# New orders in the scan, the projections and between the batches of a four-layer kernel

## The chip, the cores and the metric

The kernel runs on 1 core of one Trainium2 chip. The metric is the device time of one execution in microseconds (us), and three runs of the kernel before gave 5660.36, 5663.77 and 5664.23 us. One further execution was taken by the hardware profiler; its times are used for the working. The engines are called as in the profile: PE is TensorE's matmul, PEld its weight load, DVE is VectorE, ACT is ScalarE, POOL is GpSimd, SP is SyncE, whose queue issues most DMAs here. A "q" behind an engine (SPq) is that engine's sequencer, issuing a DMA or waiting.

## The reference

All arrays are float32; the activation x has the shape [4, 128, 128, 128] (batch, rows, columns, channels). Four layers follow each other, each with a residual and a group norm over four channels in front:

```python
x = x + _L0_conv_ref(_gn(x), w_off, b_off, w_def)   # deformable 3x3 convolution, relu
x = x + _L1_conv_ref(_gn(x), W)                     # a scan over the rows
x = x + _L2_conv_ref(_gn(x), Wself, Wm, Wk)         # three products that use sums over rows, columns
x = x + _L3_conv_ref(_gn(x), ...)                   # gated triangle product
```

Layers 1 to 3, cut to what the change touches:

```python
def step(carry, row):                               # layer 1: row after row
    new = row + relu(conv1d_same(carry, W))         # 9 taps, 128 to 128 channels
    return (new, new)

z = einsum('bmkd,hd->bmkh', x, Wself) \
    + einsum('bmd,hd->bmh', x.sum(2), Wm)[:, :, None] \
    + einsum('bkd,hd->bkh', x.sum(1), Wk)[:, None]  # layer 2

xn = layer_norm(x)                                  # layer 3
left = (xn @ left_w + left_b) * sigmoid(xn @ lgate_w + lgate_b)
right = (xn @ right_w + right_b) * sigmoid(xn @ rgate_w + rgate_b)
out_gate = sigmoid(xn @ ogate_w + ogate_b)
out = einsum('bkjd,bkid->bijd', left, right)
out = (layer_norm(out) * out_gate) @ to_out_w + to_out_b
```

## The kernel before

The program has three stages that hardly overlap. `deform_layer` computes layer 0. It ends with a test whether some offset was larger than one (`far`, L757 to L769); a branch on it, `tc.If`, would run a general version instead. `scan_layer` computes layer 1. `message_and_triangle` computes layers 2 and 3, batch after batch. In all three the order on every engine is the order in which the program writes the instructions down (`manual_schedule`), so an instruction that waits holds whatever stands behind it on its engine.

The scan works on one row of all 4 batches at a time, 128 rows in all; a carry tile holds the row split into three column phases and the three sums of phases (L1141 to L1143, `kept` 3 to 5). Per row PE does 18 convolution products into `edge_ps` and `m_ps` (L1081) and four transposes of the next row (L1061); ACT copies one product (L1111) and scales the next row (L1068); DVE combines the products (L1117 to L1134: e, y0, the new phase 0, f, y2, phase 2, e+f, y1, phase 1), makes the three sums, adds the residual into `x2c` (L1145) and takes statistics of it (`stats`, L1150); POOL adds the row to `sum_h` (L1148). Every fourth row SP stores four batches to `x2T`. After the last row DVE sums all statistics (L1154 to L1157).

Then the weights of the last layers are loaded by ACT's and SP's queues, folded and multiplied into `wcat` (L1196 to L1251), and `prelude(0)` makes the factors of layer 2's norm (mean, variance, `ws`, messages `z`). `sums_of(b)` computes layer 2 into the tile X, four rows of x2 in one step: one product of 512 columns on PE (L1359), four additions on DVE into X (L1370), one squaring on ACT (L1377). x2 comes in pieces of 32 rows, 2 MB, into two buffers R (`fetch`, L1347); a piece is fetched into a buffer after the last product that read it. `turned(b, g)` scales and transposes 32 columns of X and counts them; ahead of it `kept_columns` stores the raw columns to `x3d` (L1431; group 0 in `means`, group g+1 in the third block of group g). `spread(b, g)` norms them and makes the gate, stored to `gates`.

`projected(b, q, ...)` makes a quarter q of left and right: 8 columns in one block, 8 products (L1539), a sigmoid on ACT (L1543), two multiplications on DVE (L1545) into L and R[q % 2], written with channel steps of 128 elements. `triangle(b, q)` multiplies R and L per channel (L1557, ACT copies the result into L as L4, L1561). The R buffers thus serve the projections and x2 in turn.

At the turn from a batch to the next the order is: quarter 3 of the projections woven with triangle 2 and `prelude(b + 1)`; `fetch`; triangle 3 by itself; `counted_out(b, 0)` (statistics of the output, L1572, then the factors) woven with the first 6 steps of the next batch's `sums_of` and `turned` (the list `ahead`, 47 steps); `given(b)` woven with the rest. `given` gives the output: its step k stores the result of k-3, loads the gate of k+1 and the x3 columns of k (SP, L1638, L1586, L1591; three buffers each), norms four columns (DVE, ACT), transposes and scales (L1615, L1617), multiplies by the gate on POOL (L1618), and multiplies by `outw` on PE (L1629). `weave` interleaves lists in proportion to their lengths.

Of the kernel before, what the change touches and what calls it, by code (L numbers as in the profile page):

```python
# [19 lines left out]
B = 4  # L20
# [12 lines left out]
DQ = P // NQ  # L33

# [145 lines left out]
def deform_layer(tc, c, small, x, w_off, b_off, w_def, x1, tabs, offs):  # L180
# [14 lines left out]
    with ExitStack() as ctx:  # L195
# [552 lines left out]
        for _ in convs:  # L748
            pass
        count(len(to_count))  # L750
        beside["norms"].append(x1_norm(B - 1, stats))
        while step(B, S):
            pass


# [4 lines left out]
        nc.vector.scalar_tensor_tensor(most, ends[:, 1:2], -1.0, ends[:, 0:1], ALU.mult, ALU.max)  # L760
        most_ps = ps_g.tile([1, 2 * NL], F32, name="most_ps", tag="gn_ps")
# [7 lines left out]
        nc.vector.tensor_copy(far, row)  # L769
        return norms, far  # L770
# [240 lines left out]
def scan_layer(tc, c, small, x1, w, norms, x2T):  # L1011
# [4 lines left out]
    WP = N + 5  # L1016
    counted = small.tile([P, B, 2], F32, name="counted2")
    sum_w = small.tile([P, B, S], F32, name="sum_w")
    sum_h = small.tile([P, B, S], F32, name="sum_h")
    with ExitStack() as ctx:  # L1020
# [5 lines left out]
        ps_m = ctx.enter_context(tc.tile_pool(name="l1ps_m", bufs=1, space=PSUM))  # L1026

        stats = wp.tile([P, B, S, 6], F32, name="stats2")
# [14 lines left out]

        carry = [wp.tile([P, 2 * PHASES, B, WP], F32, name=f"carry_{i}") for i in range(2)]
# [40 lines left out]

        order = {getattr(mybir.EngineType, e) for e in ("PE", "Activation", "DVE", "Pool", "SP")}
        ctx.enter_context(tc.manual_schedule(engines=order))
        chunks = {0: rows(0), RB: rows(RB)}
        px = turned(0)
        ready = {0: (px, scaled(px))}  # L1090
        add, less = ALU.add, ALU.subtract
        for y in range(S):
# [7 lines left out]
            if y:  # L1100
                pa = ps_a.tile([P, B, N + 1], F32, name="edge_ps")
                product(pa, [(less2, old[:, 0], 1), (taps[:, 0], old[:, 2], 0)])
                ps = {}
                for name, wgt, at in (
                    ("m1", taps[:, 1], 1), ("m01", both["w12"], 3), ("m12", both["w01"], 4),
                    ("m012", both["w012"], 5),
                ):
                    ps[name] = ps_m.tile([P, B, N], F32, name=f"{name}_ps")
                    product(ps[name], [(wgt, old[:, at], 1)])
                m1 = two.tile([P, B, N], F32, name="m1")  # L1110
                nc.scalar.copy(m1, ps["m1"])  # L1111
            if y + 1 < S:
                pn = turned(y + 1)
                ready[y + 1] = (pn, scaled(pn))
            if y:
                e = two.tile([P, B, N], F32, name="e")
                nc.vector.tensor_tensor(e, ps["m01"], m1, less)  # L1117
                y0 = two.tile([P, B, N], F32, name="y0")
                nc.vector.tensor_tensor(y0, pa[:, :, 0:N], e, add)  # L1119
                nc.vector.scalar_tensor_tensor(  # L1120
# [3 lines left out]
                nc.vector.tensor_tensor(f, ps["m12"], m1, less)  # L1124
                y2 = two.tile([P, B, N], F32, name="y2")
                n2 = COUNT[2]
                nc.vector.tensor_tensor(y2[:, :, 0:n2], f[:, :, 0:n2], pa[:, :, 1 : 1 + n2], less)
                nc.vector.scalar_tensor_tensor(  # L1128
                    kept(new, 2), y2[:, :, 0:n2], 0.0, part(rt, 2), ALU.max, add
                )  # L1130
                nc.vector.tensor_tensor(e, e, f, add)
                y1 = two.tile([P, B, N], F32, name="y1")
                nc.vector.tensor_tensor(y1, ps["m012"], e, less)  # L1133
                nc.vector.scalar_tensor_tensor(  # L1134
# [5 lines left out]
            if y + 1 < S:  # L1140
                nc.vector.tensor_tensor(kept(new, 3, N), kept(new, 0, N), kept(new, 1, N), add)  # L1141
                nc.vector.tensor_tensor(kept(new, 4, N), kept(new, 1, N), kept(new, 2, N), add)
                nc.vector.tensor_tensor(kept(new, 5, N), kept(new, 3, N), kept(new, 2, N), add)  # L1143
            for p in range(PHASES):
                nc.vector.tensor_tensor(  # L1145
                    x2c[:, :, i, p:S:PHASES], part(px, p), kept(new, p), add
                )
            nc.gpsimd.tensor_tensor(sum_h, sum_h, x2c[:, :, i], add)  # L1148
            for b in range(B):
                nc.vector.bn_stats(stats[:, b, y, :], x2c[:, b, i])  # L1150
# [3 lines left out]
        nc.vector.tensor_tensor(sum_w, stats[:, :, :, 1], stats[:, :, :, 4], add)  # L1154
        nc.vector.tensor_scalar(sum_w, sum_w, S / 2.0, None, ALU.mult)
        for b in range(B):
            nc.vector.bn_aggr(counted[:, b], stats[:, b].rearrange("p n s -> p (n s)"))  # L1157
# [17 lines left out]
def message_and_triangle(tc, c, x2T, x3d, gates, counted, w2, w3, out):  # L1175
# [5 lines left out]
    wself_T, wm_T, wk_T = w2  # L1181
    (norm_g, norm_b, left_w, left_b, right_w, right_b, lgate_w, lgate_b, rgate_w, rgate_b,
     ogate_w, ogate_b, onorm_g, onorm_b, to_out_w, to_out_b) = w3
# [3 lines left out]
    QB = 8  # L1187
    QC = 4 * DQ
    FIRST = 6
    NW = NQ * QC  # L1190
    with ExitStack() as ctx:
        wp = ctx.enter_context(tc.tile_pool(name="l3w", bufs=1))

        def column(v, name):
            t = wp.tile([P, 1], F32, name=name)
            nc.scalar.dma_start(t, v.rearrange("(p o) -> p o", o=1))  # L1196
            return t

        wself = wp.tile([P, P], F32, name="wself")
        nc.scalar.dma_start(wself, wself_T)  # L1200
        wm = wp.tile([P, P], F32, name="wm")
        nc.scalar.dma_start(wm, wm_T)
        wk = wp.tile([P, P], F32, name="wk")
        nc.scalar.dma_start(wk, wk_T)
        gcol = column(norm_g, "gcol")
        bcol = column(norm_b, "bcol")
        og = column(onorm_g, "og")
        ob = column(onorm_b, "ob")
        outb = column(to_out_b, "outb")
        outw = wp.tile([P, P], F32, name="outw")  # L1210
        nc.scalar.dma_start(outw, to_out_w)

        wcat = wp.tile([P, NW + P], F32, name="wcat")
        with tc.tile_pool(name="l3prep", bufs=1) as prep, tc.tile_pool(
            name="l3ps_w", bufs=2, space=PSUM
        ) as ps_w:
            raw = prep.tile([P, NW + P], F32, name="wraw")  # L1220
            braw = prep.tile([1, NW + P], F32, name="braw")
            blocks = raw[:, 0:NW].rearrange("p (q n e) -> p q n e", q=NQ, n=4)
            bblocks = braw[:, 0:NW].rearrange("p (q n e) -> p q n e", q=NQ, n=4)
            both = ((left_w, left_b), (right_w, right_b), (lgate_w, lgate_b), (rgate_w, rgate_b))
            for n, (wgt, bias) in enumerate(both):
                nc.scalar.dma_start(blocks[:, :, n, :], wgt.rearrange("p (q e) -> p q e", q=NQ))
                nc.sync.dma_start(
                    bblocks[:, :, n, :], bias.rearrange("(o q e) -> o q e", o=1, q=NQ)
                )
            nc.scalar.dma_start(raw[:, NW:], ogate_w)  # L1230
            nc.sync.dma_start(braw[:, NW:], ogate_b.rearrange("(o n) -> o n", o=1))
            less = prep.tile([P, P], F32, name="less")
            nc.vector.tensor_copy(less, c.ident)
            nc.vector.memset(less[0:1, :], -1.0)
            nc.vector.memset(less[:, 0:1], 0.0)
            first = prep.tile([P, P], F32, name="first")
# [530 lines left out]
```

## Time and profile before

| what | value |
|---|---|
| three timed runs | 5660.36, 5663.77, 5664.23 us |
| profiled execution | 5650.97 us, of it a span of 5649.2 us |
| PE, DVE, ACT, POOL busy over the span | 92%, 57%, 49%, 14% |
| layer 0 with the branch | 0 to about 3339 us |
| scan, first row to last | about 3345 to 4094.7 us |
| from there to the first addition into X (L1370) | to 4136.8 us |
| triangle 3 of batch 0, 1, 2, 3 starts at | 4429.4, 4802.5, 5177.2, 5536.9 us |

The span is counted from the first to the last instruction. A share of busy time over the whole span hides that the stages have different limits, so what follows reads stretches. In the timeline each line has the start, the length, the engine, the line and the operation with its shapes and count; in brackets stands idle time before it and what ended it. A table of stretches has, for PE, PEld, DVE, ACT and POOL, the busy us and the instructions, then the granted TensorE clock, the DMA share and GB/s. The chain of waits is followed back from the last instruction and lists, in order of time, the work that nothing else covered.

### The profile page before, as it was taken

What the parts mean: (1) busy time and instruction counts of PE and PEld (TensorE: products, weight loads), DVE (VectorE), ACT (ScalarE), POOL (GpSimd) and SP (SyncE); (2) the same over time, 40 slices, a digit from 0 to 9 for tenths busy, and PEclk for the clock granted to TensorE, in tenths of its full rate; (3) what the DMA queues carried; (4) which work ended last, traced back from release to release, by engine and by line L of the source; (5) the groups of instructions that cost most, each with busy time, mean ns of one, the idle gap of its engine ahead of it and who ended that gap; (6) DMA issues with size and microseconds to landing.
All of it is one profiled execution on the core that took longest, in us unless ns stands there. A gap on an engine that the chain in (4) does not pass through costs nothing. (4 is left out here: it accounts for less than half of the span.)

```text
span 5649.2 us, 112077 instructions
## 1 busy us (share of the span) xinstructions
PE 5192.2 (92%) x42401; PEld 4451.7 (79%) x42401; DVE 3219.9 (57%) x10323; ACT 2767.7 (49%) x5890; POOL 779.4 (14%) x674
## 2 busy tenths in 40 slices
PE   2899999999999999999999979999969889788897
PEld 1678888888888888888888879999938668567686
DVE  5554444554444644444433349999965664765755
ACT  1355554455554455554544423333255574664755
POOL 2021111001120011111100002222200110200202
PEclk9899999999999999999999989999979899999999
DMA  4555555555554555554543422222231440722615
GB/s 147 139 136 132 137 126 117 126 122 137 132 135 109 125 137 127 137 132 104 119 80 71 79 55 91 90 90 90 86 151 38 157 182 25 258 96 82 241 46 170
DMA packets 1132346, 671.45 MB, mean 119 GB/s; under 512 B 736461, under 2 KB 1002894, under 8 KB 1113366
## 3 DMA queue, kind: packets, MB, share of 16 engines
q1 hardware_dynamic: 1121650, 657.77, 43.9%
q8 instruction: 338, 5.54, 0.4%
q10 hardware_dynamic: 10148, 6.43, 0.4%
q14 instruction: 210, 1.72, 0.1%
HBM read 382.88 MB, written 281.11 MB: 118 GB/s over the span
## 5 line engine op out<-in xcount | busy, mean ns | idle before, releaser
L509 DVE TENSOR_TENSOR m<-ty,t_ps 120x390 f32<-120x390 f32 x1548 | 804.5, 557 | 1497.3 <-ACT ty L507 1495.9
L520 PEld LDWEIGHTS v_ps<-m,pixels 120*128 120x128 f32 x11352 | 1433.6, 193 | 85.7 <-issue 8.0
L520 PE MATMUL v_ps<-m,pixels 120*128 120x108 f32 (+1 forms) x11352 | 1459.6, 273 | 3.6 <-ACT v L530 3.5
L530 ACT COPY v<-v_ps 128x432 f32<-128x432 f32 x1376 | 718.8, 522 | 1268.2 <-PE v_ps L520 1265.2
L578 PE MATMUL conv_ps<-v,wdef 128*128 128x128 f32 (+2 forms) x5160 | 1301.7, 378 | 7.0 <-DVE x1c L551 5.6
L578 PEld LDWEIGHTS conv_ps<-v,wdef 128*128 128x128 f32 x5160 | 813.1, 192 | 256.6 <-issue 21.1
L507 ACT COPY ty<-t_ps 120x390 f32<-120x390 f32 x1560 | 688.1, 489 | 180.9 <-PE t_ps L497 173.5
L497 PE MATMUL t_ps<-places,spread 25*120 25x99 bf16 (+1 forms) x10836 | 520.6, 260 | 66.3 <-DVE m L509 40.5
L497 PEld LDWEIGHTS <-spread 25*120 25x120 bf16 x10896 | 339.3, 136 | 228.3 <-issue 126.1
L1539 PEld LDWEIGHTS proj_ps<-wcat,X 128*128 128x128 f32 x4096 | 478.9, 194 | 28.7 <-issue 27.7
L1539 PE MATMUL proj_ps<-wcat,X 128*128 128x128 f32 x4096 | 487.8, 278 | 1.7 <-DVE R L1545 0.4
L392 POOL TENSOR_TENSOR off<-off,koff 72x512 f32<-72x512 f32 x128 | 162.1, 1266 | 2294.4 <-DVE off L389 2200.8
L1068 ACT ACTIVATE rowT<-x1T_ps,t_x,s_x 128x128 f32<-128x128 f32 x512 | 192.6, 457 | 367.1 <-PE x1T_ps L1061 344.0
L1545 DVE TENSOR_TENSOR L<-proj_ps,work 128x256 f32<-128x256 f32 x256 | 154.5, 603 | 382.2 <-ACT work L1543 382.2
L1081 PE MATMUL m_ps<-carry,w 128*128 128x172 f32 x2286 | 361.3, 310 | 0.0
L1618 POOL TENSOR_TENSOR work<-work,gate 128x512 f32<-128x512 f32 x128 | 163.2, 1275 | 1385.3 <-DVE X L1370 620.3
L1081 PEld LDWEIGHTS m_ps<-carry,w 128*128 128x128 f32 x2286 | 345.5, 188 | 0.0
L1148 POOL TENSOR_TENSOR sum_h<-sum_h,x2c 128x512 f32<-128x512 f32 x128 | 162.3, 1268 | 1163.6 <-DVE x2c L1145 1163.6
L1543 ACT ACTIVATE work<-proj_ps 128x512 f32<-128x512 f32 x256 | 151.1, 597 | 310.4 <-PE proj_ps L1539 310.4
L1629 PE MATMUL out_ps<-outw,work 128*128 128x128 f32 x1024 | 194.6, 292 | 23.3 <-POOL work L1618 21.8
L1359 PE MATMUL self_ps<-R,ws 128*128 128x512 f32 x256 | 150.0, 684 | 56.9 <-DVE X L1370 50.3
L1629 PEld LDWEIGHTS out_ps<-outw,work 128*128 128x128 f32 x1024 | 165.7, 203 | 34.6 <-POOL work L1618 34.4
(231 smaller groups left out, 6537.8 us busy)
## 6 DMA issues: line engine op xcount, KB each, us to landing
pixels<-tab SPq DMA_DIRECT2D x688, 123.8 KB
xin<-in_x_dram SPq DMA_DIRECT2D x56, 1024.0 KB
off<-parts SPq DMA_DIRECT2D x64, 891.0 KB
tab<-rows SPq DMA_DIRECT2D x384, 128.0 KB
places<-off SPq DMA_DIRECT2D x688, 55.7 KB
x<-x1c SPq DMA_DIRECT2D x32, 1024.0 KB
x1rows<-x SPq DMA_DIRECT2D x128, 256.0 KB
x2T<-x2c SPq DMA_DIRECT2D x128, 256.0 KB
```

Of the source, the lines that this page charges most:

```text
L497: nc.tensor.matmul(to, lhsT=spread[p0 : p0 + KROWS, ph, :], rhs=mov, start=True, stop=True,)
L507: nc.scalar.copy(ty[:, 0:n], tp[0:LANES, 0, 0:n])
L509: nc.vector.tensor_tensor(m, ty[:, 0:n].rearrange("p (r c) -> p r c", c=PADW), tx, ALU.mult)
L520: nc.tensor.matmul(vp[:, h * n : h * n + rows * w].rearrange("p (k c) -> p k c", c=w), lhsT=pix[0:LANES, xb, :], rhs=m[:, :, RX * xb : RX ...
L530: nc.scalar.copy(v[:, :, c0 : c0 + 4 * RX].rearrange("p k (h c) -> p k h c", c=RX), vp[:, 0 : 4 * n].rearrange("p (h k c) -> p k h c", h=4 ...
L578: nc.tensor.matmul(pc[:, at : at + r1 - r0, :], lhsT=wdef[:, 3 * ky + kx, :], rhs=v[:, k0 + kx, r0:r1, kx : kx + S], start=m == 0, stop=m ...
L1068: nc.scalar.activation(rt[:, b, :], px[:, b, :], AF.Identity, bias=t, scale=s)
L1081: nc.tensor.matmul(to, lhsT=wgt, rhs=src[:, :, at : at + n], start=i == 0, stop=i + 1 == len(todo),)
L1148: nc.gpsimd.tensor_tensor(sum_h, sum_h, x2c[:, :, i], add)
L1539: nc.tensor.matmul(pp[:, j], lhsT=X[:, j0 + j, :], rhs=wcat[:, cols], start=True, stop=True)
L1618: nc.gpsimd.tensor_tensor(a, a, gt, ALU.mult)
L1629: nc.tensor.matmul(po[:, j], lhsT=a[:, j], rhs=outw, start=False, stop=True)
```

## The change

Six things are changed.

1. **Branch.** The test `far` is computed before the last convolutions are drained and before the last norm, no longer after them.
2. **Scan rows.** The statistics of row y's `x2c` are taken one row later, one of the four after each of four instructions of the chain on DVE; `e + f` comes ahead of phase 2; the residual additions stand between the others. Statistics are kept for 16 rows and summed up per 16 rows (`summed`), with a small closing computation after the last row.
3. **Weights.** The weights of the last layers are loaded by ACT's queue at the start of the scan (`later.load`, 19 DMAs ahead of the first row), folded on POOL after row 4 (`later.fold`), and multiplied on PE in rows 8 and 10 into a buffer of `ps_x` (`later.product`). The two R buffers exist from the scan on, and rows 0 to 63 of x2 of batch 0 are loaded into them in rows 65 and 67.
4. **x2 in pieces.** `fetch` loads 8 rows (0.5 MB) and not 32. The next batch's rows are fetched as triangles 2 and 3 free R, later ones as `sums_of` frees them.
5. **Turn of the batch.** Triangle 3 is woven with 5 steps of `ahead`, `counted_out(b, 0)` with the next 5, `given` with the remaining 37. `given` stores after its loads. `factors` is split: the square root on ACT is issued in one step and DVE's reciprocal in a later step. `kept_columns(b, 1)` moves from the third block of `turned(b, 0)` to its end.
6. **Projection.** The sigmoid is written with columns innermost, and DVE's two multiplications run over columns innermost: they read PSUM in steps of 128 elements and write runs of 8 elements.

```diff
+        most_ps = ps_g.tile([1, 2 * NL], F32, name="most_ps", tag="gn_ps")
...
+        count(len(to_count))
+        beside["norms"].append(x1_norm(B - 1, stats))
+        while step(B, S):
+            pass
...
+        def summed(ch, i):
+            if ch < 0:
+                return
+            now = stats[:, ch % 2]
+            if i < B:
+                nc.vector.bn_aggr(parts_of[:, i, ch], now[:, i].rearrange("p n s -> p (n s)"))
+            to = sum_w[:, :, ch * CH : (ch + 1) * CH]
+            if i == B:
+                nc.vector.tensor_tensor(to, now[:, :, :, 1], now[:, :, :, 4], add)
+            if i == B + 1:
+                nc.vector.tensor_scalar(to, to, S / 2.0, None, ALU.mult)
...
         chunks = {0: rows(0), RB: rows(RB)}
+        later.load(prep)
...
+            if y in (2 * RB, 2 * RB + 2):
+                px2 = ps_x.tile([P, B, S], F32, name="x1T_ps")
+                later.product((y - 2 * RB) // 2, px2.rearrange("p b s -> p (b s)"))
...
                 nc.vector.tensor_tensor(e, ps["m01"], m1, less)
+                count(1)
                 y0 = two.tile([P, B, N], F32, name="y0")
                 nc.vector.tensor_tensor(y0, pa[:, :, 0:N], e, add)
+                count(1)
...
+                count(1)
                 y2 = two.tile([P, B, N], F32, name="y2")
...
+                nc.vector.tensor_tensor(e, e, f, add)
...
+                summed_up(0)
...
+            summed_up(2)
+            kept_sum(3, 0, 1)
+            count(1)
+            kept_sum(4, 1, 2)
+            summed_up(1)
+            kept_sum(5, 3, 2)
...
+            summed(y // CH - 1, y % CH)
+            if y == RB:
+                later.fold(prep)
+            if y in (S // 2 + 1, S // 2 + 3):
+                i = (y - S // 2) // 2
+                nc.sync.dma_start(later.R[i], x2T[0, :, i * DQ : (i + 1) * DQ, :])
...
+    def product(part, pw):
+        at = slice(512 * part, min(512 * (part + 1), WCAT))
+        n = at.stop - at.start
+        nc.tensor.matmul(pw[:, :n], lhsT=w.less, rhs=w.gained[:, at], start=True, stop=False)
+        nc.tensor.matmul(pw[:, :n], lhsT=w.first, rhs=w.raw[:, at], start=False, stop=True)
+        nc.scalar.copy(w.wcat[:, at], pw[:, :n])
+        nc.gpsimd.tensor_tensor(w.wcat[0:1, at], w.wcat[0:1, at], w.braw[:, at], ALU.add)
...
-    FIRST = 6
+    FIRST = 5
...
-                if at + JB == DQ and y0 + DQ < S:
-                    fetch(b, y0 // DQ + 2)
+                if k and y0 % PIECE == 0:
+                    fetch(b, (y0 + 2 * DQ) // PIECE - 1)
...
-                if k == 2 and g + 1 < NG_J:
+                if k == 2 and 0 < g and g + 1 < NG_J:
                     kept_columns(b, g + 1)
...
                 count(JG // JB - 1)
-                known["x", b, g] = factors(stats, "x")
+                if g == 0:
+                    kept_columns(b, 1)
+                known["x", b, g] = factors(stats, "x")()
...
-                        to[:, :, j0 : j0 + QB].rearrange("p d j -> p j d"),
-                        pp[:, :, n * DQ : (n + 1) * DQ], sig[:, :, n * DQ : (n + 1) * DQ], ALU.mult,
+                        to[:, :, j0 : j0 + QB], pp[:, :, es].rearrange("p j d -> p d j"),
+                        sig[:, es], ALU.mult,
...
+            def refill(d0):
+                if q >= NQ - 2 and d0 and d0 % PIECE == 0:
+                    fetch(b + 1, ((q - NQ + 2) * DQ + d0) // PIECE - 1)
...
-                if 3 <= k:
-                    store(k - 3)
                 if k == 0:
                     load(0)
                 if k + 1 < n:
                     load(k + 1)
                 if k < n:
                     load_x3(k)
+                if 3 <= k:
+                    store(k - 3)
...
-            fetch(b + 1, NQ % 2)
-            run(triangle(b, NQ - 1))
-            fetch(b + 1, 1 - NQ % 2)
 
             ahead = sums_of(b + 1) + turned(b + 1, 0) if b + 1 < B else []
-            run(weave(counted_out(b, 0), ahead[:FIRST]))
-            run(weave(given(b), ahead[FIRST:]))
+            run(weave(triangle(b, NQ - 1), ahead[:FIRST]))
+            run(weave(counted_out(b, 0), ahead[FIRST : 2 * FIRST]))
+            run(weave(given(b), ahead[2 * FIRST :]))
```

## The prediction

> **What bounds the kernel now.** The page's shares (PE 92%) mix stages, so I first cut the span into stretches, then read the timeline of each, then the chain of waits. First the scan, from its second row to its end, by the table of stretches (us, PE, PEld, DVE, ACT, POOL busy, clock, DMA share, GB/s):
>
> ```profile
> 3356.00:4094.00 738.00, 735.40 (x5049) 734.21 (x5047) 694.11 (x2406) 227.76 (x630) 159.87 (x127) 1.00 0.29 88
> ```
>
> PE has no idle time, and DVE is at 94%. To tell which sets the pace, one row in the timeline:
>
> ```profile
> 3707.11 1.07 PE L1081 MATMUL edge_ps<-carry,less 128*128 128x176 f32 x6
> ...
> 3708.05 0.40 DVE L1134 SCALAR_TENSOR_TENSOR carry<-y,rowT 128x172 f32<-128x172 f32 x1
> ...
> 3708.93 1.06 PE L1081 MATMUL m_ps<-carry,wconv 128*128 128x172 f32 x6
> ...
> 3712.94 1.07 PE L1081 MATMUL edge_ps<-carry,less 128*128 128x176 f32 x6
> ```
>
> A row takes 3712.94 - 3707.11 = 5.83 us. PE's 36 products start 0.15 us apart (six in 0.90) and its 4 transposes take 0.43: 36 x 0.15 + 0.43 = 5.83. So PE is back to back. Phase 1 of the carry is ready at 3708.45 and PE starts on it at 3708.93: DVE is 0.5 us ahead. PE sets the row; DVE is nearly as long, but hidden.
>
> Second, from the last row to the first addition into X, 42 us with PE at 8.8 us of work:
>
> ```profile
> 4096.47 14.05 DVE L1157 BATCH_NORM_AGGREGATE counted<-stats 128x2 f32<-128x768 f32 x4
> ...
> 4119.04 0.29 ACT L86 ACTIVATE std_x<-gp_var,eps 128x1 f32<-128x1 f32 x1 [29.94 <-DMA wraw<-in_lgate_w_dram]
> ...
> 4127.33 28.93 SPq L1347 DMA_DIRECT2D R<-x2T  x4
> ...
> 4136.80 1.21 DVE L1370 SCALAR_TENSOR_TENSOR X<-self_ps,z 128x128 f32<-128x128 f32 x4 [7.98 <-PE self_ps L1359]
> ```
>
> It is a plain chain: statistics, the norm, whose square root stands on ACT behind the issues of the weights' DMAs, folding, x2 itself.
>
> Third, the turn of a batch. For batch 1 from `given` on, nothing is full, and the chain of waits shows four long transfers. SP's timeline shows what had been issued just before each:
>
> ```profile
> 4829.00:4932.00 103.00, 77.44 (x489) 60.05 (x490) 78.76 (x297) 74.54 (x163) 33.78 (x27) 0.96 0.80 281
> ```
>
> ```profile
> 4827.49 8.53 DMA gate<-gates
> ...
> 4850.84 8.14 DMA gate<-gates
> ...
> 4902.23 8.12 DMA x3cols<-x3d
> ...
> 4924.15 6.17 DMA gate<-gates
> ```
>
> ```profile
> 4827.12 0.32 SPq L1347 DMA_DIRECT2D R<-x2T  x1
> ...
> 4849.95 0.32 SPq L1347 DMA_DIRECT2D R<-x2T  x1
> ...
> 4898.66 0.86 SPq L1431 DMA_DIRECT2D x3d<-X  x2
> ...
> 4918.10 0.96 SPq L1431 DMA_DIRECT2D x3d<-X  x2
> ```
>
> A gate of 0.25 MB queues behind 2 MB of x2 or of raw columns.
>
> **Branch: +1 us (-4 to +4).** `far` leaves the chain: 3331.05 to 3332.85, 1.8 us, and the 6.1 us from there to the first scan instruction (3338.90) can pass while the norm still runs. The rows of x1, issued at 3339.17 and landing by 3345.1, may come up to 8 us earlier. But 19 DMA issues now stand on ACT between the filter's load and the scaling of row 0. Fourteen like them took 4110.60 to 4119.0, 0.6 us each: 11.4 us. ACT, free of the norm at 3330.7, passes the branch about 3336.7 (the same 6 us) and scales from about 3348.5; it did from 3348.07. What the earlier branch gives, the weights' issues take back.
>
> **Scan rows: 0 (0 to +80 us).** The same 19 instructions stand on DVE. From the row's timeline, an instruction that needs the one in front starts 0.37 us after it, one that doesn't 0.25 (products and sums), 0.31 (phases), 0.27 (x2c), 0.20 (statistics). In the new order nearly every instruction has another between it and what it needs: 6 x 0.25 + 3 x 0.31 + 3 x 0.27 + 3 x 0.25 + 4 x 0.20 = 4.8 us, from 5.8. The chain must meet PE: counted from e's start, which follows m01's product, phase 0 is done at 1.3, phase 2 at 2.6, phase 1 at 3.45, while PE comes to them at 1.95, 2.87 and 3.77. It fits by 0.3 us, and PE keeps its 5.83 us: 127 rows gain nothing. The freed DVE time is worth nothing, as PE had no wait. The 6 summing instructions per 16 rows fit into the free 1 us (aggregates of 96 elements: a line through 0.23 us at 48, L149, and 3.51 at 768 gives 0.45). If nothing overlapped, the mean durations (0.34, 0.39, 0.38, 0.33, 0.28) add up to 6.45 us: 0.63 x 127 = +80.
>
> A rule of the Trainium skill speaks for that end: in "VectorE: DVE Perf Modes", section "The DRAIN you can't avoid", the next op doesn't start until the pipe is empty, so spreading dependent ops would gain nothing. The trace says otherwise for independent ones: f (L1124) starts at 3706.20 while phase 0 (L1120), begun at 3705.90, still runs to 3706.30. By the rule the row would be 6.45 us and the term +80, by the trace 0.
>
> **Weights inside the scan: +3.5 us (0 to +8).** In rows 8 and 10 PE gets 4 passes of 512 and 4 of 128 columns (0.43 and 0.11 us each from L1359 and L1539: 1.7 and 0.45 us), and the transposes behind them wait for ACT's copy of the buffer, 0.6 us and 0.3 for the latency, 0.2 and 0.3 in row 10: 2.6 + 0.95 = 3.5. Below nothing is excluded, for PE is full. POOL's folding and bias additions stand behind `sum_h` (1.27 us a row, 4.5 free), ACT's copies within 70% idle time. The two early x2 loads go past x1 rows that are needed 4 rows, 23 us, later; DMAs are at 29%.
>
> **Seam: -29.5 us (-24 to -31).** After the last row's statistics (4094.7): 4 aggregates 1.8, two small sums 0.4, seven closing instructions of 0.19 (such as L1293) 1.3: 4098.2, where 4110.5 stood. Prelude without loads and folding, by its own rows: mean 0.7, variance 1.7, root and reciprocal 0.9, factors and messages 1.0, products 1.5, z and its sums 1.1, last product and `less` 1.2 = 8.1; the first product of x2 runs beside it. First addition at about 4107, not 4136.8. If x2's last stores hold X's space to about 4112, it is 24.
>
> **Projection: 0 (-10 to +20).** Nearest rows: L1561 reads PSUM in steps of 128 elements on ACT at 0.58 us for 512, as long as L1543's contiguous 0.60; L1370 writes such steps on DVE 0.28 us apart. So neither side has a large price; L1545's 0.44 us apart may become 0.39. In quarters 2 and 3 PE is the bound, which hides a gain: two blocks take 4.47 us (the chain's 4342.91 to 4347.38), while one of the two buffers is filled in 1.8 and read by ACT and DVE in 2.0, together 3.8. Two multiplications longer by 0.5 us each would break that by 0.35 us in two blocks, 0.17 a block, 128 blocks: +20.
>
> **Turn of the batch: -9 us each, three times (-33 to +3).** Pieces: at 281 GB/s 2 MB take 7.5 us, 0.5 MB 1.9; the two waits of 8.5 and 8.1 shrink by up to 5.6 each, 11.2, and 2 MB leave `given`; moving group 1's columns takes away up to 6.2. Together 17, of which I take half, since ACT (74%), DVE and PE (76%) stand close behind and take over: -9. Woven triangle: PE gets 5 x 0.86 = 4.3 us more in a stretch where it was full (8.1); `counted_out` has one row fewer (-1.3), `given` four fewer (4 x 1.15 on DVE): -1.6. Split factors: reciprocal waits of about 1.2 us a batch: -1. Against it: group 1's columns now leave at the end of `turned(b, 0)`, and the next instruction of ACT (L1464, 4948.86) must wait until their first half is stored; group 0's such wait in batch 0 was 3.83 us: +3. Behind it stand the back and gate copies, so PE waits too. Sum -8.6. All waits gone would be -33; none gone and the column wait kept, +3. Batch 0 pays the column wait alone: +2. The last batch has only the split and the order of loads (1.2 us of reciprocals, 8 us of x3cols waits in 12 pieces, part of them): -3.
>
> **Sum.** 1 + 0 + 3.5 - 29.5 + 0 - 27 + 2 - 3 = -53 us: the span 5649 becomes 5596. The profiled execution (5651) lies 13 us under the median of the runs (5663.8), so against the median 5611.
>
> **Rivals.**
> - *Only the seam counts (20%)*: the turn is held by ACT and DVE, and a stall removed there reappears at the next engine. 1 + 3.5 - 29.5 = -25: 5639. For it: 74 to 77% on three engines; against it: four named waits.
> - *The turn opens up (13%)*: nearly all the long waits vanish, -22 a batch instead of -9: 5572. For it: the DMAs' 80% share falls; against it: the same three engines.
> - *The chain on DVE becomes the row (7%)*: statistics inside the chain delay phases 2 and 1 past PE's 0.3 us. At 6.45 us a row it is +80 - 53 = +27: 5691. It makes the kernel slower from 5.83 + 53/127 = 6.25 us a row on. Against it are the overlapping starts above.
> - *Seam eaten (5%)*: loads on ACT, column waits and slower multiplications cost what the seam gives: 5664.
>
> **How the numbers follow.** The forecast (55%) is 5611. About 0.2%, 11 us, is what these runs can tell from no change. Faster: 55 + 20 + 13 = 88%; same 5%; slower 7%. The range runs from 5568, where the turn opens up, to 5645, past the seam alone; outside lie the slower case, the eaten seam and some extremes of the turn.
>
> **What would show it.** Right: rows of 5.83 us with PE at 100% and DVE near 85%; first addition into X about 13 us after the last row; triangle 3 to triangle 3 about 365 us, not 373. Wrong: rows over 5.9 us with PE idle before `edge_ps`; or gates still waiting 8 us in `given`; or L1543 and L1545's successors longer than before.

## The result, and the profile after

| | before | after |
|---|---|---|
| runs | 5660.36 to 5665.76 us, median 5664.0 (4) | 5576.2 to 5594.26 us, median 5591.58 (4) |
| ratio, 95% interval | | 0.9867 [0.9849, 0.9886] |
| profiled execution | 5650.97 us, span 5649.2 | 5593.57 us, span 5591.7 |

The kernel became faster by 72 us between the medians, where 53 were forecast; the time lies inside the range. The two profiled spans differ by 57.5 us only, because layer 0, whose code is the same but for its end, took 10.7 us longer in the execution profiled after. In the profiles of this study it took between 3315 and 3326 us. Everything below is therefore read from the lengths of the stages and not from the spans:

| stage, from the traces' first instructions of each (us) | before | after | change | forecast |
|---|---|---|---|---|
| layer 0 (to its last addition into x1c) | 3315.8 | 3326.5 | +10.7 | - |
| from there to the first copy of row 0 into the carry | 33.8 | 37.8 | +4.0 | +1 |
| 128 rows | 744.2 | 748.3 | +4.1 | +3.5 |
| last addition into x2c to the first into X | 43.0 | 13.0 | -30.0 | -29.5 |
| to the first projection of batch 0 | 77.9 | 78.4 | +0.5 | +2 |
| first projection to triangle 0, four batches | 464.5 | 451.0 | -13.5 | 0 |
| triangle 0 to triangle 3, four batches | 361.7 | 352.4 | -9.3 | 0 |
| triangle 3 to the next batch's projection, three turns | 496.1 | 477.1 | -19.0 | -27 |
| triangle 3 of batch 3 to the end | 112.3 | 107.2 | -5.1 | -3 |

First the scan after the change, by the table of stretches (span and busy us of PE, PEld, DVE, ACT, POOL, then clock, DMA share and GB/s), and one row in its timeline:

```profile
3356.00:4094.00 738.00, 728.47 (x4977) 725.13 (x4977) 604.01 (x2401) 227.16 (x629) 162.52 (x132) 0.99 0.31 95
```

```profile
3706.76 0.38 DVE L1156 SCALAR_TENSOR_TENSOR carry<-y,rowT 128x172 f32<-128x172 f32 x1
3707.06 0.33 DVE L1160 TENSOR_TENSOR f<-m_ps,m 128x172 f32<-128x172 f32 x1
...
3707.83 1.07 PE L1085 MATMUL edge_ps<-carry,less 128*128 128x176 f32 x6
...
3713.66 0.62 PE L1085 MATMUL edge_ps<-carry,less 128*128 128x176 f32 x3
```

The row is still 5.83 us (3713.66 - 3707.83). The 9.5 us that PE lacks of the stretch are mostly its beginning, for row 0 starts only at 3364.4. DVE fell from 94% of the stretch to 82%. The new kernel's DVE has a statistic (L1094) between dependent instructions, and f (L1160) starts at 3707.06 while phase 0 (L1156) runs to 3707.14.

The seam, in the timeline of the kernel after:

```profile
4113.46 1.91 DVE L1101 BATCH_NORM_AGGREGATE parts<-stats 128x2 f32<-128x96 f32 x4
...
4118.73 0.29 ACT L87 ACTIVATE std_x<-gp_var,eps 128x1 f32<-128x1 f32 x1 [11.02 <-DVE gp_var L1356]
...
4125.60 1.21 DVE L1430 SCALAR_TENSOR_TENSOR X<-self_ps,z 128x128 f32<-128x128 f32 x4 [1.31 <-PE self_ps L1419]
```

The four aggregates take 1.91 us instead of 14.05, and the square root waits for DVE's variance, no longer for a weight's DMA.

At the turns, first the stretch of 103 us that begins 26.5 us after triangle 3 of batch 1, as the one shown of before, and then the transfers in the chain of waits from batch 1 to batch 2 (start, us):

```profile
4793.80:4896.80 103.00, 84.20 (x544) 65.51 (x545) 82.74 (x302) 81.95 (x175) 38.33 (x30) 0.96 0.82 262
```

```profile
4860.55 7.05 DMA gate<-gates
...
4895.23 4.75 DMA x3cols<-x3d
...
4902.81 4.07 DMA x3d<-X
4916.30 7.29 DMA gates<-gate
```

PE did 84 us of work in it and not 77, with DMAs as busy as before. One gate load of 7 us is left where two of over 8 and one of 6 stood; in the other two turns the chain has no gate load any more, but one wait of 7 us for x3 columns in each (and one of 5 in the last). The 4 us for `x3d<-X` are new: it is the store of group 1's columns, which ACT's next scaling in place has to wait for.

### The profile page after: what moved, and what is told of

The parts are those of the page before. It is cut to its first block, busy times and chain, and to the rows that moved or that the text cites. A ratio compares the mean times of both kernels' runs of the same rounds, so it can differ in the third digit from the quotient of the medians.

```text
span 5591.7 us, 112174 instructions
## 1 busy us (share of the span) xinstructions
PE 5190.3 (93%) x42401; PEld 4449.9 (80%) x42401; DVE 3067.1 (55%) x10362; ACT 2766.6 (49%) x5892; POOL 785.0 (14%) x682
## 5 line engine op out<-in xcount | busy, mean ns | idle before, releaser
L498 PE MATMUL t_ps<-places,spread 25*120 25x99 bf16 (+1 forms) x10836 | 520.2, 260 | 61.9 <-DVE m L510 38.2
L1614 DVE TENSOR_TENSOR L<-proj_ps,work 128x256 f32<-128x256 f32 x256 | 108.7, 424 | 427.1 <-ACT work L1609 427.1
```

Of the source, the lines that this page charges most:

```text
L498: nc.tensor.matmul(to, lhsT=spread[p0 : p0 + KROWS, ph, :], rhs=mov, start=True, stop=True,)
```

## The experiments

Each kernel's ratio is to the kernel before, measured beside it on the same chip. All stage lengths are in us, from one profile of each kernel; "A" is first projection to triangle 0, "Q" triangle 0 to triangle 3, each the sum of four batches, "T" the three turns.

| kernel | ratio [95%] | to row 0 | rows | seam | A | Q | T | last |
|---|---|---|---|---|---|---|---|---|
| before | 1 | 33.8 | 744.2 | 43.0 | 464.5 | 361.7 | 496.1 | 112.3 |
| after | 0.9867 [0.9849, 0.9886] | 37.8 | 748.3 | 13.0 | 451.0 | 352.4 | 477.1 | 107.2 |
| old projection | 0.9925 [0.9901, 0.9948] | 37.6 | 749.6 | 13.0 | 470.5 | 357.5 | 477.2 | 108.3 |
| new projection alone | 0.9951 [0.9934, 0.9968] | 33.3 | 744.6 | 43.3 | 450.6 | 350.7 | 494.8 | 112.4 |
| triangle alone | 0.9869 [0.9852, 0.9885] | 38.2 | 749.4 | 13.0 | 450.0 | 352.4 | 481.7 | 107.2 |
| pieces of 32 rows | 0.9901 [0.9883, 0.9918] | 37.2 | 748.5 | 13.0 | 447.6 | 350.8 | 485.4 | 108.0 |
| columns back | 0.9878 [0.9862, 0.9895] | 37.3 | 749.7 | 13.0 | 449.9 | 352.4 | 478.5 | 107.8 |
| halves undone | 0.99 [0.9882, 0.9919] | 37.6 | 749.6 | 13.0 | 451.5 | 352.4 | 485.2 | 112.6 |
| old row order | 0.9905 [0.9889, 0.9922] | 37.2 | 764.8 | 13.0 | 454.6 | 352.4 | 474.4 | 106.5 |
| old order, summed at the end | one run | 38.0 | 749.7 | 26.0 | 450.4 | 352.4 | 476.8 | 108.1 |
| light, new order | one run | 37.3 | 640.7 | 13.0 | 453.5 | 352.4 | 476.3 | 108.2 |
| light, old order | one run | 37.7 | 756.3 | 13.0 | 451.6 | 349.1 | 477.6 | 108.3 |
| weights on SP | 0.9873 [0.9855, 0.989] | 29.6 | 748.9 | 13.0 | 448.7 | 352.4 | 479.9 | 108.3 |
| SP, end, split | 0.9845 [0.9831, 0.9859] | 26.5 | 746.9 | 13.0 | 453.2 | 352.4 | 480.3 | 107.6 |

How far a stage moves by itself can be read from the kernels in which its code is the same: T lies between 474.4 and 480.3, A (new layout) between 447.6 and 454.6, the rows between 748.3 and 749.7, the last stretch between 106.5 and 108.3. So a difference of 5 us in T is at the edge of what one profile shows. The intervals of the ratio are clear of the change's only for the two projection kernels and for the old row order; the other parts rest on the stage lengths.

### The projection: taken out of the new kernel, put into the old one

```diff
-                sig = two.tile([P, 2 * DQ, QB], F32, name="work", tag="work")
-                nc.scalar.activation(
-                    sig, pp[:, :, 2 * DQ :].rearrange("p j n -> p n j"), AF.Sigmoid
-                )
+                sig = two.tile([P, QB, 2 * DQ], F32, name="work", tag="work")
+                nc.scalar.activation(sig, pp[:, :, 2 * DQ :], AF.Sigmoid)
...
-                        to[:, :, j0 : j0 + QB], pp[:, :, es].rearrange("p j d -> p d j"),
-                        sig[:, es], ALU.mult,
+                        to[:, :, j0 : j0 + QB].rearrange("p d j -> p j d"),
+                        pp[:, :, n * DQ : (n + 1) * DQ], sig[:, :, n * DQ : (n + 1) * DQ], ALU.mult,
```

> The kernel after the change, with the projection's sigmoid and its two multiplications laid out as before. In the changed kernel's trace the stretches from a batch's first projection to its first triangle take 451 us in all four batches (464.5 before), those from first to fourth triangle 352 (362 before): 23 us that the prediction put at 0. Theory: the layout won them; multiplications of 0.60 us instead of 0.42 make both sums go back to about 464 and 362, the turns stay near 477 for three, and the ratio to the kernel before rises from 0.987 to about 0.991 (+23 us). Rival: the layout is hidden by PE, as predicted, and the gain came from the order of loads and columns; then both sums stay at 451 and 352 and the ratio at 0.987.

> The kernel before the change, with the new layout of the projection alone. Theory: projections win by themselves: 464.5 + 362 becomes about 804 (-23 us), nothing else moves, ratio 0.996. Rival: hidden by PE, ratio 1.000 and the two sums unchanged. Third: DVE's freed time also shortens the turns, where groups of the projection are not run; that would show as three turns under 496 and a ratio below 0.995.

Without the layout A + Q rose from 803.4 to 828.0 (+24.6); with the layout alone they fell from 826.2 to 801.3 (-24.9), and the turns moved by 1.3 us or less in both. The layout is the cause. The group of the multiplications, in the kernel before and after (count, busy us, mean ns, idle in front):

```profile
L1545 DVE TENSOR_TENSOR L<-proj_ps,work 128x256 f32<-128x256 f32 x256 | 154.5, 603 | 382.2 <-ACT work L1543 382.2
```

```profile
L1614 DVE TENSOR_TENSOR L<-proj_ps,work 128x256 f32<-128x256 f32 x256 | 108.7, 424 | 427.1 <-ACT work L1609 427.1
```

DVE still waits most of its time for ACT, so its 180 ns saved would be worth nothing if PE always had other work in front. There are three kinds of places where it has none.

First, in Q, `prelude(b + 1)` is woven into quarter 3, and PE has to wait for small DVE instructions of it that stand behind the multiplications. The chain of waits in the kernel before (batch 1), and in the one with the new layout alone (batch 0, at the same clock of 1.00):

```profile
4764.89 0.60 ACT work L1543
4765.52 0.58 DVE L L1545
4766.10 0.43 DVE R L1545
4767.20 0.38 PE gn_ps L1296 x2
```

```profile
4386.32 0.42 DVE L L1548
4386.74 0.33 DVE R L1548
4387.77 0.38 PE gn_ps L1296 x2
```

The sigmoid and both multiplications stand uncovered ahead of the prelude's variance: 1.01 us of multiplications against 0.75. PE's waits for three such steps (L1296, L1315, L1327) were 2.4, 1.9 and 2.7 us and became 2.2, 1.5 and 2.5; triangle 3's wait for the last multiplication of the quarter fell from 1.8 to 1.5.

Second, at the end of A, the last eight blocks ahead of triangle 0 follow each other with nothing else for PE to do. In batch 2, the sigmoids of a block and of the next but one, before and with the layout alone:

```profile
5072.06 0.60 ACT L1543 ACTIVATE work<-proj_ps 128x512 f32<-128x512 f32 x1 [1.19 <-PE proj_ps L1539]
...
5076.00 0.60 ACT L1543 ACTIVATE work<-proj_ps 128x512 f32<-128x512 f32 x1 [1.19 <-PE proj_ps L1539]
```

```profile
5059.80 0.60 ACT L1543 ACTIVATE work<-proj_ps 128x512 f32<-128x512 f32 x1 [1.19 <-PE proj_ps L1539]
...
5063.44 0.60 ACT L1543 ACTIVATE work<-proj_ps 128x512 f32<-128x512 f32 x1 [1.19 <-PE proj_ps L1539]
```

Two blocks took 3.94 us and then 3.64. From the first of the eight blocks to triangle 0 it was 15.6 us in three batches and 15.8 in one, and became 14.5 and 14.8, all at a granted clock of 1.00: 1.1 us a batch.

Third, in the rest of A, PE waits for DVE again and again: in batch 2, with 4968.37 to 5083.80 before and 4958.64 to 5070.48 with the layout alone, the group of transposes that follow the norm shows it.

```profile
L1508 PE MATMUL back_ps<-ident,normed 128*128 128x128 f32 x96 | 18.8, 299 | 5.4 <-DVE normed L1499 4.2 <-ACT gate L1518 1.1
```

```profile
L1508 PE MATMUL back_ps<-ident,normed 128*128 128x128 f32 x96 | 18.6, 303 | 3.7 <-DVE normed L1499 3.4
```

The norm (L1499) stands behind the multiplications in DVE's order, so a shorter multiplication brings the norm forward. PE's wait falls from 5.4 to 3.7 us, where this part of A became 2.5 us shorter in all.

A part of the numbers in A and Q is the clock. In the table of stretches, Q of batch 0, 1 and 2 in the kernel before:

```profile
4332.68:4429.40 96.72, 87.92 (x716) 86.81 (x717) 37.53 (x85) 36.39 (x60) 0.00 (x0) 0.93 0.03 11
...
4712.07:4802.53 90.46, 81.65 (x716) 80.54 (x717) 37.59 (x85) 36.38 (x60) 0.00 (x0) 1.00 0.04 12
5083.80:5177.17 93.37, 84.57 (x716) 83.46 (x716) 37.51 (x85) 36.39 (x60) 0.00 (x0) 0.96 0.03 11
```

The same work takes 90.46 us at a granted clock of 1.00 and 96.72 at 0.93. Shorter stretches show what such a mean is made of: in batch 0 the clock was 0.50 from 4387.5 to 4394.4 and from 4414.9 to 4421.7, and 1.00 in the rest; in batch 2 it was 0.50 once, from 5162.4 to 5169.2; in batch 1 never. At equal clock (1.00) Q is 90.5 to 90.8 us with the old layout and 89.0 with the new one, and in the last batch 81.1 to 81.8 and 80.5 to 80.6. A is 115.4 to 116.0 with the old layout and 111.6 to 112.2 with the new one where the clock was 0.985 in both (0.9852 and 0.9847), and 117.7 to 118.5 and 114.4 to 115.1 where it was 0.956. So of some 25 us, 4 x 3.3 to 3.8, 3 x 1.5 to 1.8 and about 1, some 18 to 22, stay at equal clock. Why the clock falls in one batch and not in the next stays open.

### The turn of the batch, part by part

```diff
-            run(weave(triangle(b, NQ - 1), ahead[:FIRST]))
-            run(weave(counted_out(b, 0), ahead[FIRST : 2 * FIRST]))
-            run(weave(given(b), ahead[2 * FIRST :]))
+            run(triangle(b, NQ - 1))
+            run(weave(counted_out(b, 0), ahead[:FIRST + 1]))
+            run(weave(given(b), ahead[FIRST + 1 :]))
```

> The kernel after the change, with triangle 3 run by itself again and the next batch's first sums woven into the counting and what follows. Theory: the weaving is worth 1.6 us a batch, so three turns go from 477 to about 482 us, ratio 0.988. Rival: it is the larger part of the turn's 19 us, since it takes the first sums out of the stretch where DMAs are full; then three turns go to about 490 and the ratio to 0.989 or more.

Three turns took 481.7 us, +4.6, or 1.5 a batch: the theory's size, and the rival's 490 is excluded. But it is only 1.4 us above the longest of the turns whose code is the same (480.3), and the ratio shows nothing, so that the weaving is worth anything is hardly shown.

`fetch` and its three callers as before the change, 2 MB at a time:

```diff
-                    R[y0 // DQ % 2][:, at : at + PIECE, :], x2T[b, :, y0 : y0 + PIECE, :]
+                nc.sync.dma_start(R[i % 2], x2T[b, :, i * DQ : (i + 1) * DQ, :])
```

> The kernel after the change, with x2 loaded by 32 rows again. Theory: pieces carry most of the turn's gain: three turns go from 477 to about 488 us, and the gate loads behind a 2 MB transfer take 8 us again; ratio 0.989. Rival: the transfers are hidden by ACT, DVE and PE in the turn; then turns stay at 477, within 3 us, with the longer gates in the trace, ratio 0.987.

The turns took 485.4 us, +8.3 where 11 were expected, and gates of 8.3 and 8.6 us are back in the chain of waits of that kernel:

```profile
4801.32 8.32 DMA gate<-gates
...
5166.09 8.57 DMA gate<-gates
```

So the pieces are worth 2.8 us a batch, give or take 1 by the spread of T.

```diff
-                if k == 2 and 0 < g and g + 1 < NG_J:
+                if k == 2 and g + 1 < NG_J:
...
-                if g == 0:
-                    kept_columns(b, 1)
```

> The kernel after the change, with the raw columns of group 1 stored early in the turning of group 0 again, as before the change. Theory: the late store costs its wait at the start of each batch's first stretch, and saves less in the turn than was forecast: first stretches go from 451 to about 440 us in all (2.5 us a batch less), three turns from 477 to about 483, ratio near 0.986. Rival: the late store is what shortened the turns; then three turns go to 490 or more and the ratio to 0.989.

The turns took 1.4 us more and A 1.1 less. Neither the theory's gain in A nor the rival's loss in T came: the move of group 1's columns is worth nothing that these profiles can show. The wait of 4 us for group 1's store is gone from the turns in that kernel's chain of waits, and gate loads of 4.8 to 7.9 us stand in them instead.

The last one computes the factors in one piece, weaves all steps of `given` again and stores ahead of the loads:

```diff
-            return [lambda k=k: block(k) for k in range(JG // JB)] + [begin, close]
+            return [lambda k=k: block(k) for k in range(JG // JB)] + [close]
...
+                if 3 <= k:
+                    store(k - 3)
...
-                if 3 <= k:
-                    store(k - 3)
```

> The kernel after the change, with the factors of the output's norm computed in one piece, their step woven as before, and a store ahead of the loads in each step. Pieces took 8.3 us of the three turns' 19, the woven triangle 4.6, the columns 1.4. Theory: the halves and the order of loads are the rest, so the three turns go from 477 to about 482 us and the last stretch from 107.2 to 112, ratio 0.989. Rival: the pieces cover for the late loads; then turns stay within 2 us.

T grew by 8.1 us, the last stretch by 5.4, as much as the last stretch had gained. This is 2.7 us in a turn, and 5.4 in the last batch, which has no work of a next batch for cover. How it divides between the halves and the order of loads and stores was not tried. The four parts by themselves give 8.3 + 4.6 + 1.4 + 8.1 = 22.4 us of T, the change 19.0: no more apart than the spread of T. The turns were not compared at equal clock; it was 0.91 to 0.94 in them before and 0.94 after.

### The scan: what the order on DVE is worth

The old order of a row (products, phases, three sums, three additions, then four statistics) in the new kernel:

> The kernel after the change, with DVE's instructions of a scan row in the old order, statistics right behind the sums. Theory: PE sets the row at 5.83 us in either order; rows stay at 748 us within 3 us, ratio 0.987. Rival: the new order gives the row slack that the larger number of small summing instructions needs; then rows take 760 us or more and PE waits before the edge product.

The rows took 764.8 us, 16.5 more, so the theory fell and the rival stood. The next kernel keeps the old order and takes the summing of the statistics out of the rows again:

```diff
-    CH = 16
+    CH = S
```

> The kernel after the change, with DVE's scan row in the old order and with the statistics of all 128 rows summed after the last one, as before the change. With the old order alone the rows took 764.8 us. Theory: the 16 us more are the summing instructions (six in every 16 rows), for which the old order has no room; so the rows go back to 748 us (plus or minus 2), and the seam grows from 13.0 to about 25 us, as four aggregates of 768 elements take 14.05 us instead of 1.9. Rival: the old order itself delays PE in this kernel; then the rows stay at 760 or more.

The rows went back to 749.7 us, the seam grew by 13.0. So the 16.5 us are the summing, and the rows of the kernel with the old order show it one by one: rows 16 to 21, in which a chunk of 16 rows is summed, take 6.21 to 6.36 us from one e to the next instead of 5.83, and the few rows behind them 5.77. That is 2.3 us in each of 7 chunks, 16 us, for which the old order, at 5.74 us of 5.83, has no room. The new order gives them room: there rows 16 to 21 take 5.83 us.

How much room, the next two show: the last of three taps is left out of every product of the scan, so that it computes another convolution and PE needs less than DVE.

```diff
-            todo = [(wgt[:, a], src, at + a) for wgt, src, at in terms for a in range(PHASES)]
+            todo = [(wgt[:, a], src, at + a) for wgt, src, at in terms for a in range(PHASES - 1)]
```

> The kernel after the change, with the last of three taps left out of every product of the scan (so its convolution is another one): PE has 24 products of 0.15 us a row and four transposes, 4.0 us. Theory: now DVE sets the row, at 4.8 to 5.1 us by the spacings of the new order; the rows take 610 to 650 us. Rival: DVE's dependent instructions run strictly one after another, with 6.45 us a row; then rows stay near 5.8 us or above, 740 us, whichever order DVE has.

> The same, with the last tap left out of every product of the scan, and with DVE's row in the old order. Theory: DVE sets the row at 5.8 us, so the rows take 735 to 750 us; the difference to the new order, about 100 us, is what the new order freed and PE hides in the full kernel. Rival: the order doesn't matter; both take the same.

The rows took 640.7 and 756.3 us. One row in the timeline of the light kernel with the new order, and of the one with the old:

```profile
3707.67 0.37 DVE L1172 SCALAR_TENSOR_TENSOR carry<-y,rowT 128x172 f32<-128x172 f32 x1
...
3712.62 0.38 DVE L1172 SCALAR_TENSOR_TENSOR carry<-y,rowT 128x172 f32<-128x172 f32 x1
```

```profile
3707.65 0.32 DVE L1151 TENSOR_TENSOR e<-m_ps,m 128x172 f32<-128x172 f32 x1
...
3713.39 0.32 DVE L1151 TENSOR_TENSOR e<-m_ps,m 128x172 f32<-128x172 f32 x1
```

4.95 us against 5.74: the order frees 0.8 us a row, and with the summing 115 us in all would appear if PE were not the bound. PE hides all but the 16. DVE still waits about 0.3 us for PE's product ahead of e in many rows of the light kernel with the new order, so its own row is at most 4.95 us.

### Row 0, and a version that takes more

```diff
-        nc.scalar.dma_start(t, v)
+        nc.sync.dma_start(t, v)
```

and so for all 19 loads of the weights:

> The kernel after the change, with the 19 loads of the last layer's weights issued by SP, behind the eight loads of rows, instead of by ACT ahead of row 0's scaling. Theory: ACT's issues (3346.58 to 3362.8) are what row 0 waits for; its rows have landed by about 3355, so row 0 starts 8 to 10 us sooner: the stretch from layer 0 to row 0 goes from 37.8 to 28 to 30 us, ratio from 0.987 to 0.985. Rival: the transfers, not the issues, fill the queues, so that rows of x1 or the filter land later; then the stretch stays above 35 us.

In the kernel after, ACT issues from 3346.58 on, and its first scaling comes at 3362.84:

```profile
3346.00 10.15 SPq L1056 DMA_DIRECT2D x1rows<-x  x8
...
3362.49 0.30 ACTq L1268 DMA_DIRECT2D braw<-in_ogate_b_dram  x1
3362.84 2.90 ACT L1072 ACTIVATE rowT<-x1T_ps,t_x,s_x 128x128 f32<-128x128 f32 x8 [21.03 <-DMA wraw<-in_rgate_w_dram]
```

With the weights on SP it waits for the rows alone:

```profile
3337.97 6.98 SPq L1056 DMA_DIRECT2D x1rows<-x  x8
...
3346.64 2.91 ACT L1072 ACTIVATE rowT<-x1T_ps,t_x,s_x 128x128 f32<-128x128 f32 x8 [12.78 <-DMA x1rows<-x]
```

From SP's first issue to the scaling it is 8.7 us, where it was 16.8; the stretch fell by 8.2 us to 29.6, the theory's size. On the whole time (0.9873 against 0.9867) 8 us don't show.

The last kernel adds two edits: row 0 of x1 is loaded ahead of rows 1 to 3, and the products of the folded weights move behind the last row.

```diff
+            for r0, r1 in ((0, 1), (1, RB)) if y0 == 0 else ((0, RB),):
...
-            if y in (2 * RB, 2 * RB + 2):
+        for i in range(2):
+            px2 = ps_x.tile([P, B, S], F32, name="x1T_ps")
+            later.product(i, px2.rearrange("p b s -> p (b s)"))
```

> The kernel after the change with three edits: the weights' loads on SP, row 0 of x1 loaded by itself ahead of rows 1 to 3, and the two products of the folded weights computed behind the last row, while PE waits for the statistics, instead of in rows 8 and 10. Theory, by the stretches of the changed kernel: to row 0 from 37.8 to about 26 us (8 from the issues, as measured, 3 to 4 from the smaller first load), rows from 748.3 to 744.3, seam 13.0 unchanged because PE is idle there: 16 us in all, ratio 0.984. Rival: the products' copies on ACT and the bias on POOL delay the norm's square root or the first addition, so the seam grows by the 4 us that the rows lose, and the smaller load lands no sooner; then 8 us, ratio 0.9855.

To row 0: 26.5 us, -11.3 in all. Seam: 13.0, so the products are free there. Rows: 746.9, -1.4 instead of -4. Rows 8 and 10, which took 8.43 and 6.84 us in the kernel after, take 5.83 here, so moving the products gave 3.6 us. But from the first copy of row 0 to row 1's e it is now 8.0 us and not 5.8: row 0 starts before rows 1 to 3 have landed, PE waits 1.2 us for them, and its granted clock there was 0.57 and not 0.71. The median is 5575.69 us (5 runs), 16 us under that of the change, the ratio 0.9845 [0.9831, 0.9859]. The stages show the gain of 13 us; the intervals of the two ratios, from different chips, overlap.

## Why the prediction was right, and where not

**Branch, +1: measured +4.0, the size of one term was off.** That ACT's issues take back what the earlier branch gives is shown by the weights on SP (-8.2). The prediction priced 19 issues at 0.6 us, 11.4 us; they took from 3346.58 to 3362.79, 16.2 us, 0.85 each.

**Scan rows, 0: right, but by half a reason.** PE sets the row (5.83 us). The forecast of DVE's row, 4.8 us, was 4.95 at most in the light kernel; the end of +80 us, instructions one after the other, is excluded by it. The section that the prediction names for that end also says that a next op that is not held starts earlier, so it doesn't stand against the trace. What the prediction didn't see is that "fit into the free 1 us" is the whole worth of the new order: without it the summing costs 16.5 us.

**Weights inside the scan, +3.5: measured +4.1.** Rows 8 and 10 show it by themselves: 8.43 and 6.84 us instead of 5.83 are 2.6 + 1.0, of it 1.0 us of waits for ACT's copies, and in the last kernel, without products in them, both are back at 5.83.

**Seam, -29.5: measured -30.0.** Statistics summed at the end put 13.0 us back (12.3 by the prediction's steps, 4110.5 - 4098.2). The other 17, the norm's root no longer behind the weights' loads and the folding, follow from the timeline and were not tried alone.

**Projection, 0 (-10 to +20): wrong, -22.8; some 18 to 22 at equal clock.** The step that failed is "PE is the bound, which hides a gain". It was worked out for quarters 2 and 3, where the products of a triangle stand between the blocks and two blocks take 4.47 us. It left out A: its last eight blocks have no triangle between them, and there the cycle of the two buffers, which the prediction had at 3.8 us, was the pace at 3.94 and became 3.64; and in the rest of A, PE waits for a norm that stands behind the multiplications on DVE. In quarter 3 it left out the prelude's steps and triangle 3, which wait for multiplications without cover. One of its inputs was off too: the spacing of two multiplications fell from 0.44 to 0.34 us and not to 0.39. The Trainium skill has a rule that bears on it and that the prediction did not weigh: "SBUF — State Buffer", section "Door 1: The DMA port swizzle (why `[64,N]` ≈ `[32,N]`)", says that SBUF is read and written in lines of 16 bytes and that every step to a new line pays. The old layout wrote every element 512 bytes from the last, the new one runs of 32 bytes, and 603 ns became 424. Which of the operands made the difference was not tried.

**Turn, -9 each: measured -6.3.** (Half of 17 is 8.5, with which the prediction's terms give -8.1.) Its parts were mis-sized in both directions, as far as the spread of T lets one say. Pieces and columns, halved to 8.5, gave 2.8 + 0.5; split factors, with the order of loads, gave 2.7 instead of 1; the woven triangle gave 1.5 of 1.6, hardly clear of the spread. The column wait (+3) is there, 4.1 us in the chain, yet moving the columns back gained nothing. **Batch 0**, +2, was +0.5, and the **last batch**, -3, was -5.1.

**The sum.** +4.0 + 4.1 - 30.0 + 0.5 - 22.8 - 19.0 - 5.1 = -68.3 us outside layer 0, against -53: the projection's 23 us were missed and 8 us of the turn over-counted, so the sum lies nearer than its parts do. Its signs came: rows of 5.83 us, DVE at 82%, the first addition into X 13.0 us behind the last row, and 362 and 365 us from triangle 3 to triangle 3 in the first two turns. Of the rivals, "only the seam counts" (5639), the eaten seam and the chain on DVE fell; "the turn opens up" gave a time (5572) near the result for a reason that didn't hold, as the turns gave 6 us each and not 22.

## What to carry to other kernels

An engine that waits most of its time can still be worth shortening: look for the places where its work has no cover: at the junction of two phases, where blocks follow each other with no other work between them, and where another engine's input stands behind it in program order. Reordering a hidden engine pays nothing by itself, but it makes room; ask what the same change puts into that room. When shares differ between two profiles, compare stages at equal granted clock, for here one stage took 90.5 or 96.7 us with the same work.

## What the runs showed of the hardware

- DVE's product of 256 elements a partition took 0.60 us when it wrote SBUF in steps of 512 bytes and read PSUM contiguously, 0.42 when it wrote runs of 32 bytes and read PSUM in steps. ACT's sigmoid took 597 ns for 512 elements in either layout.
- The same 19 DMA issues took 16.2 us on ACT, beside the loads of rows, and 11.4 us on SP behind them (3345.12 to 3356.50). SP's own eight issues beside ACT's took 10.15 us, alone 6.98.
- With independent instructions between dependent ones a row of the light kernel took 4.95 us instead of 5.74.
- In this kernel on one core the granted clock of one and the same stage was 0.93, 1.00 and 0.96 in successive batches: 1.00 but for stretches of 6.8 us at 0.50, two of them, none and one.
